# First transfers in another order, leftover taps as a whole-tile product, distances of two groups together

## The chip, the cores and the metric

The kernel runs on one core of a Trainium2 chip. The time is what the device takes for one execution, in microseconds (us); of several runs the median is given. The engines are named as in the profile: PE is the matrix engine (TensorE), PEld its weight loads, DVE the vector engine, ACT the scalar engine, POOL is GpSimd, and SP the engine that mostly issues transfers (DMAs).

## The reference, cut to what matters

Two graph layers work on 128 graphs of 128 nodes with 256 features, all in float32. Each is followed by a residual and a layer norm.

```python
# layer 0
norm  = (sum(adj, -1) + 1e-6) ** -0.5
f_hom = adj @ ((x @ theta) * norm) * norm
f_het = x @ W_h
gate  = sigmoid(x @ W_t + b_t)
x     = layernorm(x + elu(gate * f_hom + (1 - gate) * f_het))
# layer 1; xc = x transposed: channels, nodes
h      = relu(bn1(conv1d(xc, conv1_w)))             # one tap
x_conv = relu(bn2(conv1d(h, conv2_w, pad=8)) + xc)  # 17 taps over the nodes
s      = x @ w_se.T + b_se                          # three coordinates per node
dist   = sq[:, None] + sq[None, :] - 2 * s @ s.T    # sq: squared length of s
msg    = relu(x @ w_msg.T + b_msg)
x_nmp  = (exp(-dist) * adj) @ msg
x      = layernorm(x + gru([x_conv, x_nmp], x))     # gates r, z, n
```

The adjacency is dense in form: 128 matrices of 128x128.

## The kernel before

There are three stages.

**Stage A** (to about 720 us) goes over the 64 pairs of graphs in a loop over t, with each pair's work spread over several rounds: `l0_turn(t+1)` transposes the inputs (xT_ps) and sums degrees (deg), `l0_project(t)` makes f_ps and gate_ps, `l0_mix(t)` applies the adjacency (mix_ps), `l1_turn(t-2)` transposes the normed result (x1T_ps), `l1_front` is the one-tap convolution, and `l1_analyse` turns its result into coefficients over 136 frequencies (coef_ps). The 17-tap convolution is done as products per frequency. Therefore the weights conv2_w have to be turned into frequencies too, and stage A does this beside its other work. `w_load`, `w_unit` and `w_store` do 128 of the 136 rows, with four groups of 17 taps on four 32-row parts of PE (w_ps). `v_load`, `v_unit` and `v_store` do the leftover eight. There, seven input channels at a time (FS = 7, 7 x 17 = 119 rows) are multiplied with TL, a table with blocks for each channel (wl_ps, 56 rows out), in 19 units. TL is put together in `way_back` from table T by 14 small DMAs that POOL issues (L247). The layer norm's and the degree's power of -1/2 (`inv_sqrt`, L161 and L162) is also on POOL.

What sets the order: up to round 2 a scheduler decides, except on PE, where the order written in the code holds; from round 3 on the code's order holds for PE, SP, DVE and ACT. [...] Before the first round, SP gets `load(0)`, the gate weights, conv1's weights, `load(1)`, `w_load(0)` and `w_load(1)`. `load(p)` brings x and adjT of pair p.

**Stage B** (to about 912 us) multiplies by frequency (y_ps, z_ps).

**Stage C** (to the end) goes over 32 groups of four graphs, where PE's order is the code's and the rest is scheduled. For a group g, `l1_own` takes coordinates for the distances (every fourth group it transposes 16 graphs' worth, turn_ps, into `turned`, and each group scales them by a mask into `own`); `l1_kernel` multiplies `turned` and `own` on four 32-row parts of PE (dist_ps), takes exp(-dist) on ACT and multiplies with the adjacency on DVE (AT). `l1_project` makes the messages (msg_ps), `l1_gather` sums them by AT (nmp_ps), `l1_synth` goes back from frequencies to nodes for two groups (conv_ps), and `l1_gru` makes the gates for two graphs at a time (pr = 0, 1) in seven products (g_ps, three matmul kinds each) that go through four PSUM banks and are summed up by DVE and POOL. `l1_kernel(g + 1)` is put before the fifth product of `l1_gru(g, 1)`. Its PSUM tile takes four banks, which it shares in turn with `l1_synth`.

Of the kernel before, what the change touches and what calls it, by code (L numbers as in the profile page):

```python
# [9 lines left out]
F32 = mybir.dt.float32  # L10
I32 = mybir.dt.int32
AF = mybir.ActivationFunctionType
ALU = mybir.AluOpType

P = 128
D = 256
NC = D // P
J = 2
G = 4
TAPS = 17  # L20
# [7 lines left out]
ML = M - P  # L28
# [6 lines left out]
def gnn_layers_kernel(ctx: ExitStack, tc: tile.TileContext, a: dict, out: bass.AP):  # L35
# [10 lines left out]
    nc = tc.nc  # L46
    x, adjT = a["x"], a["adjT"]
# [35 lines left out]
    taps = actx.enter_context(tc.tile_pool(name="taps", bufs=1, side="right", reuse_waits="tile"))  # L83
# [4 lines left out]
    SL = const.tile([P, P], F32, tag="SL", name="SL")  # L88
    T = taps.tile([P, M], F32, tag="T", name="T")
    FS = P // TAPS  # L90
    TL = taps.tile([P, ML * FS], F32, tag="TL", name="TL")
    conv1_w = acon.tile([P, NC, D + CO], F32, tag="conv1_w", name="conv1_w")
    shift1 = acon.tile([P, D], F32, tag="shift1", name="shift1")
    NW = 3
    wt = [taps.tile([P, 2, D], F32, tag=f"wt{i}", name=f"wt{i}") for i in range(NW)]


# [15 lines left out]
    def load(p):  # L113
        s = st[p] = {}
        s["x"] = io.tile([P, J, D], F32, tag="x", name=f"x_{p}")
        nc.sync.dma_start(s["x"], x[p * J : (p + 1) * J].rearrange("b n d -> n b d"))
        s["adjT"] = io.tile([P, J, P], F32, tag="adjT", name=f"adjT_{p}")
        nc.sync.dma_start(s["adjT"], adjT[:, p * J : (p + 1) * J, :])
# [4 lines left out]
    def w_load(u):  # L123
        t = wt[u % NW]
        for r in range(4):
            f = r * QF + 2 * u
            nc.sync.dma_start(
                t[32 * r : 32 * r + TAPS], a["conv2_wT"][f : f + 2].rearrange("i t o -> t i o")
            )
# [16 lines left out]
    for i, q in enumerate("vmgb"):  # L146
        for k in range(2):
# [2 lines left out]
                vec[r : r + NC], a[f"L1_gnn_bn{k + 1}_{q}"].rearrange("(c p) -> c p", p=P)  # L150
            )

    nc.sync.dma_start(conv1_w[:, :, 0:D], a["conv1_wT"].rearrange("(c p) e -> p c e", p=P))
    nc.sync.dma_start(conv1_w[:, :, D:], a["w_seT"].rearrange("(c p) e -> p c e", p=P))
    load(1)
    w_load(0)
    w_load(1)

    def inv_sqrt(dst, src, eps, width):

# [74 lines left out]
    def way_back():  # L235

        AL = setup.tile([P, P // ML, ML], F32, tag="AL", name="AL")
        nc.vector.tensor_copy(AL, A[:, P:M].unsqueeze(1).to_broadcast([P, P // ML, ML]))
        nc.vector.memset(TL, 0.0)
        back = setup.tile([P, 1], F32, tag="back", name="back")  # L240
        nc.vector.memset(back, 2.0 / L)
        nc.vector.memset(back[0:2], 1.0 / L)

        cols = TL.rearrange("p (r i k) -> p r i k", r=2, i=FS)
        for i in range(FS):
            for r in range(2):
                nc.gpsimd.dma_start(  # L247
                    cols[i * TAPS : (i + 1) * TAPS, r, i, :], T[0:TAPS, P + r : M : 2]
                )
        tS = bank("S_ps")  # L250
        nc.tensor.transpose(tS[:, 0:P], A[:, 0:P], ident)
        nc.tensor.transpose(tS[:, P : 2 * P], AL.rearrange("p a b -> p (a b)"), ident)
        nc.vector.tensor_scalar(S, tS[:, 0:P], back, None, ALU.mult)
        nc.vector.tensor_scalar(SL, tS[:, P : 2 * P], 2.0 / L, None, ALU.mult)
# [185 lines left out]
    def v_sets(v):  # L440

        return [(f, min(FS, D - f)) for f in range(2 * FS * v, min(2 * FS * (v + 1), D), FS)]

    def v_load(v):
        t = taps.tile([P, 2, D], F32, tag="vt", bufs=2, name=f"v_t_{v}")
        for i, (f, n) in enumerate(v_sets(v)):
            nc.sync.dma_start(
                t[0 : n * TAPS, i, :], a["conv2_wT"][f : f + n].rearrange("i t o -> (i t) o")
            )
        s_v[v] = t  # L450

    def v_unit(v):
        n, sets = v_sets(v)[-1][1] * TAPS, len(v_sets(v))
        pl = bank(f"wl_ps_{v}")
        nc.tensor.matmul(  # L455
            pl[0 : ML * FS, 0 : sets * D], lhsT=TL[0:n],
            rhs=s_v[v][0:n, 0:sets].rearrange("p i o -> p (i o)"), start=True, stop=True,
        )
        ol = s_v[v] = taps.tile([ML * FS, 2, D], F32, tag="wl", name=f"wl_o_{v}")
        nc.vector.tensor_copy(  # L460
            ol[:, 0:sets].rearrange("p i o -> p (i o)"), pl[0 : ML * FS, 0 : sets * D]
        )
# [48 lines left out]
    for t in range(-1, NP):  # L511
        with tc.manual_schedule(engines={E.PE, E.SP, E.DVE, E.Activation} if t > 2 else {E.PE}):

            def on(q, work):
                if 0 <= q < NP:
                    work(q)

            def between():
                on(t - 1, l0_gate)
                on(t - 3, l1_analyse)  # L520

            def beside():
                on(t - 1, l0_elu)

            on(t - 2, l1_turn)
            l0_project(t, between, beside) if t >= 0 else between()
            on(t - 1, l0_norm)
            if t == 0:
                norms = batch_norms()
                next(norms)  # L530
                table(A, node, "A")
                table(T, lag, "T")

                cos, sin = T[:, 2:M:2], T[:, 3:M:2]
                both = setup.tile([P, M // 2 - 1], F32, tag="both", name="both")
                nc.vector.tensor_sub(both, sin, cos)
                nc.vector.scalar_tensor_tensor(sin, sin, -1.0, cos, ALU.mult, ALU.subtract)
                nc.vector.tensor_copy(cos, both)
            on(t - 2, l1_front)
            on(t - 2, l1_store)  # L540
            if t + 2 < NP:
                if 2 <= t + 2:
                    load(t + 2)
            else:
                m_load(t + 2 - NP)
            if t - 1 in units:
                w_store(units[t - 1])
            if t - 1 in units_v:
                v_store(units_v[t - 1])
            on(t + 1, l0_turn)  # L550
            if t == 2:
                v_load(0)
            if t == 3:
                nc.scalar.dma_start(w_msg, a["w_msgT"].rearrange("(c p) e -> p c e", p=P))
                nc.scalar.dma_start(b_msg, a["L1_gnn_b_msg"].partition_broadcast(P))
            if t == 1:
                next(norms, None)
                way_back()
                sctx.close()
                hpool = hstack.enter_context(tc.tile_pool(name="hpool", bufs=1))  # L560
                H = hpool.tile([P, NC, M, NB], F32, tag="H", name="H")
            on(t, l0_mix)
            if t in units_v:
                if units_v[t] + 1 < NV:
                    v_load(units_v[t] + 1)
                v_unit(units_v[t])
            if t in units:
                if units[t] + 2 < NU:
                    w_load(units[t] + 2)
                if t + 1 < NP:  # L570
                    w_unit(units[t])
# [299 lines left out]
        )  # L871
        st[g].update(turned=turned, own=own)

    def l1_kernel(g):
        s = st[g]
        turned, own = s["turned"], s["own"]
        pd = acc.tile([P, G, 512], F32, tag="acc", name=f"dist_ps_{g}")
        for q in range(G):
            k = slice(q * P // G, (q + 1) * P // G)
            nc.tensor.matmul(  # L880
                pd[:, q, 0:P], lhsT=turned[k, 0, :], rhs=own[k, :], start=True, stop=True
            )
        AT = ck.tile([P, G * P], F32, tag="AT", name=f"AT_{g}")
        nc.scalar.activation(
            AT.rearrange("p (q n) -> p q n", q=G), pd[:, :, 0:P], AF.Exp, scale=-1.0
        )
        nc.vector.tensor_mul(AT, AT, s["adjT"].rearrange("p q n -> p (q n)"))
        s["AT"] = AT


    def l1_gather(g):
# [115 lines left out]
    with tc.manual_schedule(engines={mybir.EngineType.PE}):  # L1007
        load_c(0)
        load_c(1)
        load_y(0)  # L1010
        for g in range(2):
            load_x1(g)
            l1_own(g)
        l1_project(0)
        l1_kernel(0)
        l1_project(1)
        l1_factors()
        l1_synth(0)
        for g in range(NG):
            d = g // 2  # L1020
            if g + 2 < NG:
                load_c(g + 2)
                if g % 2 == 0:
                    load_y(d + 1)
                load_x1(g + 2)
            l1_gather(g)
            if 2 <= g + 1 < NG:
                l1_own(g + 1)
                l1_project(g + 1)
            l1_gru(g, 0)  # L1030
            if g % 2 == 1 and d + 1 < ND:
                l1_synth(d + 1)
            if g + 1 < NG:
                l1_gru(g, 1, {4: lambda: l1_kernel(g + 1)})
    with tc.manual_schedule(engines={E.PE, E.DVE, E.Activation}):
        l1_gru(NG - 1, 1)
    cctx.close()
# [41 lines left out]
```

## Time and profile before

| | |
|---|---|
| median of three runs | 2053.21 us (2051.23 to 2053.49) |
| profiled execution | 2053.39 us |
| its span, first to last instruction | 2051.6 us |
| granted PE clock, mean | 0.995 |
| DMA rate over the span | 118 GB/s |
| PE in 0 to 50 us | 37.10 us busy, granted clock 0.86 |
| PE in 50 to 720 us (stage A) | 670.00 us busy |
| PE in 735 to 912 us (stage B) | 175.82 us busy |
| PE in 912 to 2051 us (stage C) | 1127.32 us busy |

The profile is of one execution. Busy time counts what an engine executes, not the waits; a float32 matmul of the code appears as two passes in the records. A form such as `32*128 32x128` gives the tile of the array that is used, and the streamed operand. In the view of waits, a row gives who waited for whom, the total in us, how often, and the longest.

### The profile page before, as it was taken

The page shows a single profiled execution, that of the slowest core. Times are in us where ns is not written, and L with a number is a line of the kernel's source. Part 1 is how long each engine was busy: PE and PEld are TensorE (multiplying, and loading weights), DVE is VectorE, ACT ScalarE, POOL GpSimd, SP SyncE. Part 2 cuts the span into 40 slices and gives each one's busy share as a digit, 9 for nine tenths or more (in the row PEclk, how much of TensorE's full clock was granted, in tenths as well). Part 3 has the DMA queues.
Part 4 walks back from the last instruction along what each step waited for, and adds up shares of the span by engine and source line. Part 5 has one row for each costly group of instructions (what it writes and reads, how often), then busy time and mean ns, then how long its engine had stood idle before and what let it go on. Part 6 is the DMA issues. An engine that isn't in the chain of part 4 may idle for free.

```text
span 2051.6 us, 27050 instructions
## 1 busy us (share of the span) xinstructions
PE 2023.9 (99%) x8807; PEld 1384.2 (67%) x8807; DVE 1432.1 (70%) x2882; ACT 746.4 (36%) x1488; POOL 652.0 (32%) x869
## 2 busy tenths in 40 slices
PE   7999999999999999999999999999999999999997
PEld 4666766766766788886666666666666666666664
DVE  5777777777777764456767677676667767776766
ACT  2555655655555621112222222222322222232222
POOL 4111111111111135553433334333424333342431
PEclk8999999999999999999999999999999999999999
DMA  4544444444444479994222122222212222121100
GB/s 96 170 153 149 142 154 150 141 156 152 141 153 146 133 269 359 313 306 147 72 74 79 52 66 81 63 66 64 79 61 70 73 67 63 58 79 52 42 26 21
DMA packets 198044, 243.04 MB, mean 118 GB/s; under 512 B 16768, under 2 KB 141456, under 8 KB 197904
## 3 DMA queue, kind: packets, MB, share of 16 engines
q1 hardware_dynamic: 190880, 235.47, 35.3%
q10 hardware_dynamic: 6352, 5.78, 0.9%
q0 software_dynamic: 672, 0.06, 0.4%
q8 instruction: 71, 1.16, 0.3%
q14 instruction: 69, 0.57, 0.1%
HBM read 136.33 MB, written 104.86 MB: 118 GB/s over the span
## 4 chain that ended last, share of the span: by engine, by line
PE 96%; DVE 2%; POOL 1%; DMA 1%; ACT 0%; issue 0%; POOLq 0%; DVEq 0%; ACTq 0%; SPq 0%
PE g_ps L964 42%; PE f_ps L317 11%; PE conv_ps L387 5%; PE gate_ps L322 5%; PE msg_ps L844 5%; PE y_ps L708 5%; PE mix_ps L343 3%; PE coef_ps L407 3%; PE nmp_ps L897 3%; PE conv_ps L808 3%; PE z_ps L721 3%; PE x1T_ps L284 2%; PE w_ps L423 2%; PE xT_ps L284 1%; PE deg L297 1%; PE wl_ps L455 1%
## 5 line engine op out<-in xcount | busy, mean ns | idle before, releaser
L317 PE MATMUL f_ps<-w,xT 128*128 128x512 f32 x512 | 244.4, 600 | 0.1
L923 ACT ACTIVATE o<-o 128x1024 f32<-128x1024 f32 (+1 forms) x65 | 67.8, 1044 | 326.8 <-DVE o L1000 269.7
L161 POOL TENSOR_SCALAR rstd_b<-mv_b 128x2 f32<-128x2 f32 (+1 forms) x65 | 18.2, 280 | 529.6 <-DVE mv_b L262 529.6
L964 PE MATMUL g_ps<-t_h,sh 128*128 128x384 f32 x384 | 158.4, 494 | 0.0
L964 PE MATMUL g_ps<-t_c,sc 128*128 128x384 f32 x384 | 155.2, 486 | 0.0
L964 PE MATMUL g_ps<-t_m,sm 128*128 128x384 f32 x384 | 155.2, 486 | 0.0
L161 POOL TENSOR_SCALAR rstd_a<-mv_a 128x2 f32<-128x2 f32 x64 | 12.3, 193 | 436.4 <-DVE mv_a L262 380.1
L322 PEld LDWEIGHTS gate_ps<-w,xT 128*128 128x128 f32 x512 | 98.3, 192 | 69.1 <-issue 61.8
L322 PE MATMUL gate_ps<-w,xT 128*128 128x256 f32 x512 | 132.6, 382 | 0.0
L997 POOL TENSOR_TENSOR u<-u,p 128x512 f32<-128x512 f32 x63 | 79.8, 1267 | 163.3 <-DVE p L981 163.3
L317 PEld LDWEIGHTS f_ps<-w,xT 128*128 128x128 f32 x512 | 89.0, 193 | 62.9 <-issue 62.3
L708 PE MATMUL y_ps<-wb,H 128*128 128x256 f32 x544 | 128.5, 379 | 0.9 <-ACT H L411 0.8
L326 ACT ACTIVATE hom<-f_ps,norm 128x256 f32<-128x256 f32 x128 | 60.7, 474 | 187.6 <-PE f_ps L317 182.3
L271 ACT ACTIVATE y<-y,nb_b,rstd_b 128x256 f32<-128x256 f32 x128 | 70.0, 593 | 157.8 <-DVE nb_b L269 157.8
L387 PE MATMUL conv_ps<-conv_w,x1T 128*128 128x259 f32 x512 | 122.5, 381 | 0.0
L716 POOL TENSOR_TENSOR ws<-wb 128x512 f32<-128x512 f32 x67 | 93.2, 1390 | 88.8 <-PE z_ps L721 53.5
L708 PEld LDWEIGHTS y_ps<-wb,H 128*128 128x128 f32 x544 | 103.2, 190 | 15.4 <-issue 1.4
L844 PE MATMUL msg_ps<-w_msg,cx1T 128*128 128x256 f32 x480 | 108.7, 379 | 0.0
L964 PEld LDWEIGHTS g_ps<-t_c,sc 128*128 128x128 f32 x384 | 73.0, 190 | 50.9
L964 PEld LDWEIGHTS g_ps<-t_m,sm 128*128 128x128 f32 x384 | 73.0, 190 | 50.9 <-DVE sm L912 0.2
L387 PEld LDWEIGHTS conv_ps<-conv_w,x1T 128*128 128x128 f32 x512 | 97.1, 190 | 14.7 <-ACT w_o L427 0.2
L964 PE MATMUL g_ps<-w_hhT_w,cx1T 128*128 128x384 f32 x256 | 105.0, 492 | 0.0
(228 smaller groups left out, 4524.8 us busy)
## 6 DMA issues: line engine op xcount, KB each, us to landing
wb<-w_d SPq DMA_DIRECT2D x68, 512.0 KB
w_d<-w_o SPq DMA_DIRECT2D x256, 128.0 KB
y_d<-yb SPq DMA_DIRECT2D x68, 256.0 KB
x<-in_x SPq DMA_DIRECT2D x64, 256.0 KB
cx1T<-x1T_d SPq DMA_DIRECT2D x64, 256.0 KB
yt<-y_d SPq DMA_DIRECT2D x32, 512.0 KB
cx<-x_d SPq DMA_DIRECT2D x32, 512.0 KB
x_d<-x SPq DMA_DIRECT2D x63, 256.0 KB
```

Of the source, the lines that this page charges most:

```text
L271: nc.scalar.activation(dst[:, q, :], src[:, q, :], AF.Identity, bias=nb[:, q : q + 1], scale=rstd[:, q : q + 1],)
L284: nc.tensor.transpose(t[:, (c * J + j) * P : (c * J + j + 1) * P], src[:, j, c * P : (c + 1) * P], ident,)
L317: nc.tensor.matmul(pf, lhsT=xT[:, c, nodes(j)], rhs=w0[:, c, 0 : 2 * D], start=(c == 0), stop=(c == NC - 1),)
L322: nc.tensor.matmul(pg[:, j * D : (j + 1) * D], lhsT=xT[:, c, nodes(j)], rhs=w0[:, c, 2 * D : 3 * D], start=(c == 0), stop=(c == NC - 1),)
L343: nc.tensor.matmul(pm[:, j * D : (j + 1) * D], lhsT=adjT_[:, j, :], rhs=hom[:, j, :], start=True, stop=True,)
L387: nc.tensor.matmul(ph[:, 0 : D + CO], lhsT=s["x1T"][:, c, nodes(j)], rhs=conv1_w[:, c, :], start=(c == 0), stop=(c == NC - 1),)
L708: nc.tensor.matmul(py[:, blk, :], lhsT=coefs(blk if k == 0 else 2 * k + 1 - blk, c), rhs=w[:, c, blk, :], start=(c == 0), stop=(c == NC - 1),)
L716: nc.gpsimd.tensor_tensor(ws, w[:, :, 0, :], w[:, :, 1, :], ALU.add)
L844: nc.tensor.matmul(pm[:, j * D : (j + 1) * D], lhsT=x1T[:, c, nodes(q)], rhs=w_msg[:, c, :], start=(c == 0), stop=(c == NC - 1),)
L923: nc.scalar.activation(rz, rz, AF.Tanh, scale=0.5)
L964: nc.tensor.matmul(pg[:, lo : lo + 3 * P], lhsT=s[f"f{kind}"][i][:, pr, :], rhs=factors[kind][i], start=(k == 0), stop=(k == 2), skip_grou ...
L997: nc.gpsimd.tensor_tensor(u4, u2, p5, add)
```

## The change

It has three parts.

First, `load(1)` comes before conv1's weights; `w_load(0)` and `w_load(1)` go into rounds 0 and 1, behind `load(2)` and `load(3)`; `v_load(0)` and `v_load(1)` go into rounds 2 and 3, and `v_load(v + 2)` comes after `v_unit(v)` instead of `v_load(v + 1)` before it. The `v_load` of unit v + 2 writes the buffer that unit v has just read.

Second, TL grows from 56 to 128 columns (zeros beyond the 56), the inputs get two fixed tiles `vt` whose last rows are set to zero once, and `v_unit` multiplies all 128 rows by all 128 columns; only the 56 rows of the result are read, as before.

Third, `l1_kernel` takes two groups. It puts the second group's distances in the columns beside the first's in the same four banks, and it is called for groups 0 and 1 at the start and then within `l1_gru(g, 1)` of odd g alone, for g + 1 and g + 2. `l1_own` is called one group earlier and before `l1_gather`, and AT has three buffers.

```diff
-    TL = taps.tile([P, ML * FS], F32, tag="TL", name="TL")
+    TL = taps.tile([P, P], F32, tag="TL", name="TL")
...
+    vt = [taps.tile([P, 2, D], F32, tag=f"vt{i}", name=f"vt{i}") for i in range(2)]
...
+    load(1)
     nc.sync.dma_start(conv1_w[:, :, 0:D], a["conv1_wT"].rearrange("(c p) e -> p c e", p=P))
     nc.sync.dma_start(conv1_w[:, :, D:], a["w_seT"].rearrange("(c p) e -> p c e", p=P))
-    load(1)
-    w_load(0)
-    w_load(1)
...
         nc.vector.memset(TL, 0.0)
+
+        for t in vt:
+            nc.vector.memset(t[96:], 0.0)
...
-        cols = TL.rearrange("p (r i k) -> p r i k", r=2, i=FS)
+        cols = TL[:, 0 : ML * FS].rearrange("p (r i k) -> p r i k", r=2, i=FS)
...
     def v_load(v):
-        t = taps.tile([P, 2, D], F32, tag="vt", bufs=2, name=f"v_t_{v}")
+        t = vt[v % 2]
...
     def v_unit(v):
-        n, sets = v_sets(v)[-1][1] * TAPS, len(v_sets(v))
+        sets = len(v_sets(v))
         pl = bank(f"wl_ps_{v}")
         nc.tensor.matmul(
-            pl[0 : ML * FS, 0 : sets * D], lhsT=TL[0:n],
-            rhs=s_v[v][0:n, 0:sets].rearrange("p i o -> p (i o)"), start=True, stop=True,
+            pl[:, 0 : sets * D], lhsT=TL, rhs=vt[v % 2][:, 0:sets].rearrange("p i o -> p (i o)"),
+            start=True, stop=True,
         )
...
                 if 2 <= t + 2:
                     load(t + 2)
+                if 0 <= t < 2:
+                    w_load(t)
+                if 2 <= t < 4:
+                    v_load(t - 2)
...
-            if t == 2:
-                v_load(0)
...
             if t in units_v:
-                if units_v[t] + 1 < NV:
-                    v_load(units_v[t] + 1)
                 v_unit(units_v[t])
+                if units_v[t] + 2 < NV:
+                    v_load(units_v[t] + 2)
...
-    def l1_kernel(g):
-        s = st[g]
-        turned, own = s["turned"], s["own"]
-        pd = acc.tile([P, G, 512], F32, tag="acc", name=f"dist_ps_{g}")
-        for q in range(G):
-            k = slice(q * P // G, (q + 1) * P // G)
-            nc.tensor.matmul(
-                pd[:, q, 0:P], lhsT=turned[k, 0, :], rhs=own[k, :], start=True, stop=True
+    def l1_kernel(*groups):
+
+        pd = acc.tile([P, G, 512], F32, tag="acc", name=f"dist_ps_{groups[0]}")
+        for i, g in enumerate(groups):
+            turned, own = st[g]["turned"], st[g]["own"]
+            for q in range(G):
+                k = slice(q * P // G, (q + 1) * P // G)
+                nc.tensor.matmul(
+                    pd[:, q, i * P : (i + 1) * P], lhsT=turned[k, 0, :], rhs=own[k, :],
+                    start=True, stop=True, skip_group_check=True,
+                )
+        for i, g in enumerate(groups):
+            AT = st[g]["AT"] = ck.tile([P, G * P], F32, tag="AT", bufs=3, name=f"AT_{g}")
+            nc.scalar.activation(
+                AT.rearrange("p (q n) -> p q n", q=G), pd[:, :, i * P : (i + 1) * P],
+                AF.Exp, scale=-1.0,
             )
-        AT = ck.tile([P, G * P], F32, tag="AT", name=f"AT_{g}")
-        nc.scalar.activation(
-            AT.rearrange("p (q n) -> p q n", q=G), pd[:, :, 0:P], AF.Exp, scale=-1.0
-        )
-        nc.vector.tensor_mul(AT, AT, s["adjT"].rearrange("p q n -> p (q n)"))
-        s["AT"] = AT
+            nc.vector.tensor_mul(AT, AT, st[g]["adjT"].rearrange("p q n -> p (q n)"))
...
         l1_project(0)
-        l1_kernel(0)
+        l1_kernel(0, 1)
         l1_project(1)
...
                 load_x1(g + 2)
+                l1_own(g + 2)
             l1_gather(g)
             if 2 <= g + 1 < NG:
-                l1_own(g + 1)
                 l1_project(g + 1)
...
             if g + 1 < NG:
-                l1_gru(g, 1, {4: lambda: l1_kernel(g + 1)})
+
+                l1_gru(g, 1, {4: lambda: l1_kernel(g + 1, g + 2)} if g % 2 == 1 else {})
```

More of the change, by code (lines that the diff above doesn't have):

```diff
@@ L449, in v_load @@
             )
-        s_v[v] = t
     def v_unit(v):
-        n, sets = v_sets(v)[-1][1] * TAPS, len(v_sets(v))
+        sets = len(v_sets(v))
         pl = bank(f"wl_ps_{v}")
         nc.tensor.matmul(
-            pl[0 : ML * FS, 0 : sets * D], lhsT=TL[0:n],
-            rhs=s_v[v][0:n, 0:sets].rearrange("p i o -> p (i o)"), start=True, stop=True,
+            pl[:, 0 : sets * D], lhsT=TL, rhs=vt[v % 2][:, 0:sets].rearrange("p i o -> p (i o)"),
+            start=True, stop=True,
         )
```

## The prediction

> **What bounds the kernel now.** I read the page first: the busy shares, then the chain that ended last.
>
> ```profile
> PE 2023.9 (99%) x8807; PEld 1384.2 (67%) x8807; DVE 1432.1 (70%) x2882; ACT 746.4 (36%) x1488; POOL 652.0 (32%) x869
> PE 96%; DVE 2%; POOL 1%; DMA 1%; ACT 0%; issue 0%; POOLq 0%; DVEq 0%; ACTq 0%; SPq 0%
> ```
>
> TensorE (PE) is busy for 2023.9 of 2051.6 us and makes 96% of the chain. A change can win in two ways only: it takes away PE's few waits, or it makes PE's own work shorter. So next the waits of PE, the two longest:
>
> ```profile
> PE xT_ps L284 <- DMA x<-in_x: 9.3, 2, 5.0
> PE x1T_ps L284 <- ACT x L271: 4.0, 3, 3.5
> ```
>
> Of the first row's 9.3 us, 4.3 are the start of the kernel, and 4.97 are a wait for the third pair of batches at 20.9 to 25.86 us. The 3.48 us of the second row end at 34.80. After 36 us PE hardly waits at all. To see what stands behind 34.80, the chain in order of time:
>
> ```profile
> 18.29 1.10 POOL TL L247
> 20.25 12.60 POOL TL L247 x12
> 32.93 0.20 POOL rstd_a L161
> 33.95 0.17 DVE nb_a L269
> 34.80 0.47 PE x1T_ps L284
> ```
>
> Fourteen small transfers into TL are issued by POOL, 1.06 us each, one right behind the other from 16.52 to 32.86 us, and the first layer norm's 1/sqrt on POOL is queued behind them. The third pair's late arrival is not in this chain.
>
> For PE's own work the timeline of PE. First a round with a product of leftover taps (wl_ps), then one without, where x1T follows mix at once. Columns: start, length, engine, line.
>
> ```profile
> 68.74 1.11 PE L343 MATMUL mix_ps<-hom,adjT 128*128 128x256 f32 x4
> 69.78 1.07 PE L455 MATMUL wl_ps<-v_t,TL 119*56 119x512 f32 x2
> 70.78 0.66 PE L284 MATMUL x1T_ps<-ident,x 128*128 128x128 f32 x4
> 71.27 1.88 PE L317 MATMUL f_ps<-w,xT 128*128 128x512 f32 x4
> ...
> 113.58 1.11 PE L343 MATMUL mix_ps<-hom,adjT 128*128 128x256 f32 x4
> 114.53 0.60 PE L284 MATMUL x1T_ps<-ident,x 128*128 128x128 f32 x4
> 114.96 1.88 PE L317 MATMUL f_ps<-w,xT 128*128 128x512 f32 x4
> ```
>
> From mix to f_ps it is 2.53 us with the product and 1.38 without: the product costs 1.15. Its two passes of 512 columns should cost 0.86 (f_ps, full tile: 71.27 to 72.99 for four, 0.43 each). So 0.29 us is lost at the edges where the tile goes from 128*128 to 119*56 and back. The same for the distances:
>
> ```profile
> 981.99 0.81 PE L964 MATMUL g_ps<-t_m,sm 128*128 128x384 f32 x2
> 982.73 0.50 PE L880 MATMUL dist_ps<-own,turned 32*128 32x128 f32 x8
> 983.16 0.91 PE L964 MATMUL g_ps<-t_h,sh 128*128 128x384 f32 x2
> 983.91 0.81 PE L964 MATMUL g_ps<-t_c,sc 128*128 128x384 f32 x2
> 984.55 0.81 PE L964 MATMUL g_ps<-t_m,sm 128*128 128x384 f32 x2
> ```
>
> Pairs of g_ps passes follow every 0.645 us, so 981.99 to 983.91 would take 1.29 without the distances; it takes 1.92. One group's distances cost 0.63: 0.10 on the way in, 0.43 themselves, 0.10 on the way out.
>
> **Part 1, order of the first transfers.** The second pair's x and adjacency go ahead of conv1's weights, and the first two w_loads (8 issues on SP, 7.08 us of its time from 8.59 on) go behind load(2) and load(3). SP then issues x of pair 2 near 8.6 instead of 15.72, so it is there long before PE asks at 20.73. The 4.97 us wait goes. What is late next: x1T of pair 0. PE's remaining work before it (transposes, degrees, row_ps, S_ps, mix) takes about 2.8 us, so it stands at x1T from about 23.5 us. POOL's order is unchanged; its first TL issue at 16.52 follows from the tables on DVE and from PE's vec_ps at 13.60, neither of which waits for a moved transfer. So x1T still starts at 34.80, and one wait of about 11 us stands where there were 4.97 and 3.48. Part 1 is worth 0.
>
> [...] The passes after the wait ran at half pace: xT_ps to mix_ps took 25.86 to 31.33, 5.5 us for 2.8 us of work. [...] The slow stretch after 34.80 (f_ps at 35.99 takes 3.62 for four, otherwise 1.88) stays, since PE has idled longer, not shorter. [...]
>
> What else moves: two memsets of 32x512 at the head of DVE; a DVE pass over 128x512 takes 0.69, so at most 1.4 us, against 0.89 idle there and 1.71 and 1.05 idle further on before the tables matter. The w_loads land by about 20 us and are used at 47.29 and 58.53. v_load(v+2) now waits on SP for the product v; behind it stands the store of x1T, which is copied after that product anyway. Cost 0; without the cover, a product would wait for some us once.
>
> **Part 2, whole tile for the leftover taps.** 19 products. The passes keep their 512 columns (256 in the last), so the 0.86 stays, and the 0.29 goes if a whole tile follows whole tiles as f_ps does after x1T. The longer weight load (190 ns against 128) lies under mix's pass of 216. 19 x 0.287 (the third digit from the starts of the single passes) = -5.45 us. Ends: 0 if the edges have another cause, -5.5.
>
> **Part 3, distances of two groups at once.** 16 pairs instead of 32 groups. A pair costs the edges once and four waves (of four 32-row tiles) instead of two. What is a further wave worth? The tile views of w_ps and dist_ps, the same 32-row form with 512 and 128 columns:
>
> ```profile
> L423 PE MATMUL w_ps<-wt,T x256: 587/640/692, 47.3 to 717.8; 17*128 17x512 f32 x128
> L880 PE MATMUL dist_ps<-own,turned x256: 270/321/372, 916.4 to 2004.6; 32*128 32x128 f32 x128
> ```
>
> Half the passes are longer by 105 and 102 ns: the first wave shows its weight load, the second doesn't. So a further wave costs its stream alone, 0.107 (w_ps: 0.427 for 512 columns). A pair then takes 0.10 + 0.43 + 2 x 0.107 + 0.10 = 0.846 against 2 x 0.632 = 1.265: 0.42 saved, times 16 = -6.7 us. [...]
>
> Off PE, at odd groups DVE now does two AT multiplies (0.68 each) and two own scalings (0.25 each) together before it sums product 4 (p<-g_ps, at 985.40 in the round shown). That sum ends near 987.3 instead of 986.1. PE next needs that bank for the second nmp_ps, at about 989.96: 2.7 us of cover. The two Exp on ACT take 0.60 each, and ACT idles 6.25 us after the first there. The adjacency of the second group is needed one group earlier; its load was issued at 985.29 for group 5, whose pair now comes at about 1050. The eight turn_ps pairs only move. Cost 0.
>
> **Sum.** 0 - 5.45 - 6.7 = -12.15 us. The profiled execution took 2053.39, 0.18 above the median of the runs. 2053.39 - 12.15 = 2041.2; against the median 2041.1.
>
> **Rivals.** (A) The forecast, 2041.1: 64%. (B) Loads of further waves are exposed as the rule says: 2053.2 - 5.45 - 3.3 = 2044.5: 14%. For it: the case with more than two waves in a row is not in the trace. (C) Part 1 pays, because the TL chain is not what it seems and x1T follows the third pair: up to 7.7 more, 2033.5, half of it 2037: 7%. Against it: POOL's 12.60 us without a gap. (D) The whole tile does not remove its edges, that is, the change does not do what it says: 2046.5: 6%. If the pairs fail as well, 2053: 3%. Against: mix to x1T at 113.58 shows no edge between whole tiles. (E) Slower: DVE becomes the bound in odd groups. If the two Exp come late behind an activation of 1.04 and a norm of 1.09 on ACT and the sum of product 4 is delayed by more than the 2.7 us of cover, PE waits for the bank in each of 15 pairs. It wins back all from 0.81 us of wait per pair (12.15 / 15), so from 3.5 us of lateness on; at 1.2 us it is 2053.2 - 12.15 + 18 = 2059: 6%. For it: DVE lags 5 us behind PE at 981.80, after the convolution's outputs.
>
> **Numbers.** 2041.1 is the case A. The range 2037.0 to 2046.5 holds A, B, the mild half of C and most of D. A change under 0.2% (4.1 us) can't be told from none by this measurement. Faster is A to D: 0.91; same, where both tile edits fail: 0.03; slower 0.06.
>
> **What would show it.** wl_ps should read 128*128, with x1T 0.86 us after it. dist_ps should come x16 in 16 places, 0.65 us to the next g_ps, with a third and a fourth wave as short as the second. PE's wait for x<-in_x should fall to about 4.3, that for ACT x rise to about 11, with x1T still at 34.8. It is wrong if x1T starts well before or after 34.8, if PE waits in the odd groups, or if a pair takes 0.86 or more.

## The result, and the profile after

The median went from 2052.56 us (four runs, 2051.23 to 2053.49) to 2041.52 us (four runs, 2040.12 to 2043.36). The ratio is 0.9947, with a 95% interval of 0.993 to 0.9964. The forecast was 2041.1, in a range of 2037.0 to 2046.5. The profiled execution took 2040.12 us, its span 2038.3 us, and the mean granted clock was 0.995 as before.

The page of the kernel after, its busy shares and the shares of the chain that ended last:

```profile
PE 2008.1 (99%) x8807; PEld 1387.0 (68%) x8807; DVE 1445.5 (71%) x2884; ACT 745.9 (37%) x1488; POOL 645.2 (32%) x869
...
PE 96%; DVE 2%; POOL 1%; ACT 0%; issue 0%; DMA 0%; POOLq 0%; DVEq 0%; ACTq 0%
```

PE runs the same 8807 passes in 15.8 us less of busy time (2023.9 before). It is still 96% of the chain: nothing else has become the bound. DVE has two instructions more, the two memsets.

The two longest waits of PE, of the kernel after (total, times, longest):

```profile
PE x1T_ps L286 <- ACT x L273: 11.6, 3, 11.1
PE xT_ps L286 <- DMA x<-in_x: 4.2, 1, 4.2
```

The wait for the third pair's x is gone (9.3 in two waits before, 4.2 in one after), and the wait for ACT's x has grown from a longest of 3.5 to 11.1. The chain in order of time shows where that wait ends and why:

```profile
19.73 12.58 POOL TL L249 x12
...
32.38 0.20 POOL rstd_a L160
...
32.66 0.73 POOL rstd_a L161
...
33.60 0.61 ACT x L273
...
34.25 0.47 PE x1T_ps L286
```

POOL still issues the TL transfers without a gap until 32.3 us. The first layer norm comes right behind, and x1T starts at 34.25 us, 0.55 earlier than before. The twelve issues themselves begin 0.52 earlier (19.73 here, 20.25 before).

The timeline of PE after, first a round with leftover taps, then a pair of groups' distances:

```profile
67.97 1.11 PE L345 MATMUL mix_ps<-hom,adjT 128*128 128x256 f32 x4
68.92 1.02 PE L456 MATMUL wl_ps<-vt,TL 128*128 128x512 f32 x2
69.78 0.60 PE L286 MATMUL x1T_ps<-ident,x 128*128 128x128 f32 x4
70.21 1.02 PE L319 MATMUL f_ps<-w,xT 128*128 128x512 f32 x2
```
```profile
974.83 0.81 PE L970 MATMUL g_ps<-t_m,sm 128*128 128x384 f32 x2
975.57 0.73 PE L884 MATMUL dist_ps<-own,turned 32*128 32x128 f32 x16
976.23 0.91 PE L970 MATMUL g_ps<-t_h,sh 128*128 128x384 f32 x2
976.97 0.81 PE L970 MATMUL g_ps<-t_c,sc 128*128 128x384 f32 x2
```

From mix to f_ps it is now 2.24 us (70.21 - 67.97), 2.53 before. From wl_ps to x1T it is 0.86, which is two passes of 512 columns at 0.43 each, the pace of f_ps. For the distances, 974.83 to 976.97 is 2.14 us and holds two pairs of g_ps passes (1.29), so 0.85 for two groups. Before it was 0.63 for one.

In summary, from the starts of instructions in the two traces (us):

| stretch of the profiled execution | before | after | difference |
|---|---|---|---|
| start to the first leftover product | 69.78 | 68.92 | -0.86 |
| first to last leftover product | 637.83 | 632.55 | -5.28 |
| from there to the first turn_ps of stage C | 204.95 | 204.34 | -0.61 |
| stage C, first turn_ps to last g_ps | 1126.75 | 1120.25 | -6.50 |

These add up to -13.25 of the 13.27 us between the two profiled executions; the medians are 11.04 apart. Single executions of one kernel differ by up to 6 us (2031.49 to 2037.36 in the four of the kernel after with its TL issues split), so the rows of the changed stages say more than the total. The first row is not the worth of part 1: the first leftover product starts at 68.79 us in the kernel with part 3 alone and at 69.69 in the one with part 2 alone, both with the old order of transfers.

### The profile page after: what moved, and what is told of

It is laid out like the page before. It is cut to its first block, busy times and chain, and to the rows that moved or that the text cites. A ratio compares the mean times of both kernels' runs of the same rounds, so it can differ in the third digit from the quotient of the medians.

```text
span 2038.3 us, 26961 instructions
## 1 busy us (share of the span) xinstructions
PE 2008.1 (99%) x8807; PEld 1387.0 (68%) x8807; DVE 1445.5 (71%) x2884; ACT 745.9 (37%) x1488; POOL 645.2 (32%) x869
## 4 chain that ended last, share of the span: by engine, by line
PE 96%; DVE 2%; POOL 1%; ACT 0%; issue 0%; DMA 0%; POOLq 0%; DVEq 0%; ACTq 0%
PE g_ps L970 42%; PE f_ps L319 11%; PE y_ps L711 6%; PE conv_ps L389 5%; PE gate_ps L324 5%; PE msg_ps L847 5%; PE mix_ps L345 3%; PE coef_ps L409 3%; PE nmp_ps L903 3%; PE conv_ps L811 3%; PE z_ps L724 3%; PE x1T_ps L286 2%; PE w_ps L425 2%; PE xT_ps L286 1%; PE deg L299 1%; PE conv_ps L818 1%
## 5 line engine op out<-in xcount | busy, mean ns | idle before, releaser
L160 POOL TENSOR_SCALAR rstd_b<-mv_b 128x2 f32<-128x2 f32 (+1 forms) x65 | 12.5, 192 | 529.9 <-DVE mv_b L264 529.9
```

## The experiments

The theory to test was that of the prediction. Parts 2 and 3 each pay by PE edges removed (an edge is what PE loses on its way between products of different tile form), and part 1 pays nothing, since TL's issues on POOL set the start of x1T. The rival was that part 1 pays and that the tile edits pay less. Where a median of before is given, it was measured on the same chip beside the kernel.

### One part at a time

**The first transfers alone**: the kernel before with part 1.

```diff
...
+    load(1)
     nc.sync.dma_start(conv1_w[:, :, 0:D], a["conv1_wT"].rearrange("(c p) e -> p c e", p=P))
     nc.sync.dma_start(conv1_w[:, :, D:], a["w_seT"].rearrange("(c p) e -> p c e", p=P))
-    load(1)
-    w_load(0)
-    w_load(1)
...
+                if 0 <= t < 2:
+                    w_load(t)
+                if 2 <= t < 4:
+                    v_load(t - 2)
...
-            if t == 2:
-                v_load(0)
...
-                if units_v[t] + 1 < NV:
-                    v_load(units_v[t] + 1)
                 v_unit(units_v[t])
+                if units_v[t] + 2 < NV:
+                    v_load(units_v[t] + 2)
```

> The kernel before with the first part alone, the order of the transfers. Theory (the start hangs on POOL's fourteen TL transfers): the wait for the third pair's x (4.97 us) goes, the wait at x1T grows to about 11 us, x1T of pair 0 still starts at 34.2 to 34.8 us, and the time is that of before within 0.7 us. Rival (the third pair's arrival costs 4.97 us and 2.7 us of slow clock): x1T starts near 27 to 30 us and the time falls by 5 to 7.7 us.

Measured: 2052.48 us against 2052.34 before; ratio 1.0001 [0.9993, 1.0009]. The waits of PE, and POOL's timeline:

```profile
PE x1T_ps L282 <- ACT x L269: 11.6, 3, 11.1
PE xT_ps L282 <- DMA x<-in_x: 4.3, 1, 4.3
```
```profile
20.62 12.61 POOL L245 DMA_DIRECT2D TL<-T  x12
33.30 0.19 POOL L159 TENSOR_SCALAR rstd_a<-mv_a 128x2 f32<-128x2 f32 x1
```

The 4.97 us wait is removed and comes back in front of x1T: two waits of 8.45 us together have become one of 11.05. The 2.6 us between them are the half pace of the passes from xT_ps to mix_ps (granted clock 0.50 from 24.05 to 30.87 us before), which has gone too and has been waited away as well. The twelve issues take the same 12.6 us, and the norm stands directly behind them. Part 1 alone is worth nothing, within 0.1% either way.

**The leftover taps alone**: the kernel before with part 2.

```diff
...
-            pl[0 : ML * FS, 0 : sets * D], lhsT=TL[0:n],
-            rhs=s_v[v][0:n, 0:sets].rearrange("p i o -> p (i o)"), start=True, stop=True,
+            pl[:, 0 : sets * D], lhsT=TL, rhs=vt[v % 2][:, 0:sets].rearrange("p i o -> p (i o)"),
+            start=True, stop=True,
...
```

> The kernel before with the second part alone, leftover taps by a whole tile. Theory (edges between tile shapes cost 0.287 us per product): wl_ps to x1T_ps 0.86 instead of 1.00 us, mix to wl_ps 0.216 instead of 0.309, in all 5.45 us less. Rival (the 11 us of the whole change come mostly from the pairs and the start): 0 to 2 us less.

Measured: 2047.31 us; ratio 0.9975 [0.9965, 0.9985], so about 5.1 us less. From the first to the last leftover product it is 632.55 us, to the hundredth as in the kernel with all three parts; stage C stays at 1126.75.

**The pairs alone**: the kernel before with part 3.

```diff
...
-        l1_kernel(0)
+        l1_kernel(0, 1)
...
-                l1_gru(g, 1, {4: lambda: l1_kernel(g + 1)})
+                l1_gru(g, 1, {4: lambda: l1_kernel(g + 1, g + 2)} if g % 2 == 1 else {})
```

> The kernel before with the third part alone, distances of two groups at once. Theory (a further wave of four row tiles costs its stream of 0.107 us, the edges are paid once): 0.41 us less for each of 16 pairs, 6.5 us in all. Rival (weight loads of further waves are exposed): 0.21 us per pair, 3.3 us in all. Rival (DVE in odd groups): no gain, PE waits in stage C.

Measured: 2045.92 us; ratio 0.9968 [0.9956, 0.998], so about 6.6 us less. Stage C is 1120.25 us long, the leftover products' stretch is as before. The tile view of the distances in this kernel (min/median/max of one pass, ns):

```profile
L881 PE MATMUL dist_ps<-own,turned x256: 270/270/373, 914.9 to 1964.3; 32*128 32x128 f32 x128
```

The median has gone from 321 to 270. Before, half of the passes were long (372 against 270), those of the first of two waves. Now only the first of four waves is long, and the median falls on the short ones. The records of the kernel after show the same and the weight loads with it: at 975.57 the first four loads (181 ns) start with their own passes, which take 372; the loads of the other three waves (184 to 187 ns) start while earlier passes run, and their passes take 270.

The three parts alone give about 0, -5.1 and -6.6 us, together -11.7; the whole change gave 0.53% [0.36, 0.7], or 10.9 us. They add, within what the interval allows (7 to 14 us).

### Which edge did the leftover product pay for?

Part 2 changes two sizes at once: the rows in use from 119 to 128, and the columns from 56 to 128. Each of two kernels keeps one of the old sizes.

119 rows with 128 columns, the rest as after:

```diff
-            pl[:, 0 : sets * D], lhsT=TL, rhs=vt[v % 2][:, 0:sets].rearrange("p i o -> p (i o)"),
+            pl[:, 0 : sets * D], lhsT=TL[0 : FS * TAPS], rhs=vt[v % 2][0 : FS * TAPS, 0:sets].rearrange("p i o -> p (i o)"),
```

> The changed kernel, with the leftover taps by 119 rows and all 128 columns. If the edges come from the number of columns in use (56), they stay away: mix to wl_ps 0.216 us, wl_ps to x1T_ps 0.86 us. If they come from the rows, they are back: 0.309 and about 1.00 us.

128 rows with 56 columns, the rest as after:

```diff
-            pl[:, 0 : sets * D], lhsT=TL, rhs=vt[v % 2][:, 0:sets].rearrange("p i o -> p (i o)"),
+            pl[0 : ML * FS, 0 : sets * D], lhsT=TL[:, 0 : ML * FS], rhs=vt[v % 2][:, 0:sets].rearrange("p i o -> p (i o)"),
```

> The changed kernel, with the leftover taps by all 128 rows and 56 columns. If the edges come from the columns, they are back: mix to wl_ps 0.309 us, wl_ps to x1T_ps about 1.00 us, 5.4 us in all. If from the rows, they stay away: 0.216 and 0.86 us.

Measured, one execution each: 2040.25 us for 119 x 128, 2045.74 us for 128 x 56. The timelines of PE, first of 119 x 128, then of 128 x 56:

```profile
67.66 1.11 PE L345 MATMUL mix_ps<-hom,adjT 128*128 128x256 f32 x4
68.60 1.02 PE L456 MATMUL wl_ps<-vt,TL 119*128 119x512 f32 x2
69.47 0.60 PE L286 MATMUL x1T_ps<-ident,x 128*128 128x128 f32 x4
```
```profile
68.15 1.11 PE L345 MATMUL mix_ps<-hom,adjT 128*128 128x256 f32 x4
69.19 1.07 PE L456 MATMUL wl_ps<-vt,TL 128*56 128x512 f32 x2
70.19 0.66 PE L286 MATMUL x1T_ps<-ident,x 128*128 128x128 f32 x4
```

From mix to x1T it is 1.81 us with 119 rows, the same as with the whole tile (67.97 to 69.78), and 2.04 with 56 columns, the same as before (68.74 to 70.78). With 56 columns wl_ps begins 0.10 us later after mix, x1T 0.14 later after wl_ps, and x1T itself takes 0.06 more (0.66 for 0.60). All nineteen products say the same: from the first to the last it is 632.62 us with 119 rows (632.55 with the whole tile) and 637.83 with 56 columns (637.83 before). The edge belongs to the number of columns in use. The step from 128 to 119 rows costs nothing, so the zero rows of `vt` and the two memsets could be left out. Fewer rows were not tried in this product; the distances with their 32-row tiles do have edges (0.10 us on each side in the round at 982.73 before).

### What POOL's fourteen issues cost

If TL's issues are what holds x1T back, moving them behind the norm should start x1T earlier, and more so when part 1 has brought the third pair in. Both kernels issue eight of TL's fourteen transfers in round 1 and six in round 2, with POOL's order in the first rounds as written.

```diff
+    def fill_left(lo, hi):
+        cols = TL[:, 0 : ML * FS].rearrange("p (r i k) -> p r i k", r=2, i=FS)
+        for i in range(lo, hi):
+            for r in range(2):
+                nc.gpsimd.dma_start(
+                    cols[i * TAPS : (i + 1) * TAPS, r, i, :], T[0:TAPS, P + r : M : 2]
+                )
...
-        for i in range(FS):
-            for r in range(2):
-                nc.gpsimd.dma_start(
-                    cols[i * TAPS : (i + 1) * TAPS, r, i, :], T[0:TAPS, P + r : M : 2]
-                )
+        fill_left(0, 4)
...
-        with tc.manual_schedule(engines={E.PE, E.SP, E.DVE, E.Activation} if t > 2 else {E.PE}):
+        with tc.manual_schedule(engines={E.PE, E.SP, E.DVE, E.Activation} if t > 2 else {E.PE, E.Pool}):
...
+            if t == 2:
+                fill_left(4, FS)
```

On the kernel after:

> The changed kernel, with POOL's order held to the code's in the first rounds and six of the fourteen TL transfers put into round 2, so that the first norm's 1/sqrt comes before all TL transfers. Theory (x1T waits for POOL's queue alone): x1T of pair 0 starts near 26.4 us instead of 34.25, 7.9 us less than the changed kernel, and up to 2.7 us more if PE's clock does not drop in the shorter wait; about 2033.5 us, at best 2031. Rival (something else holds x1T, or the TL transfers now hold the second norm for as long): 0 to 3 us less.

On the kernel before:

> The kernel before, its order of transfers kept, with the same new order of the TL transfers on POOL. Theory: now the third pair's x (wait to 25.86 us) is what the start hangs on, PE goes from there to x1T without a second wait, at about 31.3 us instead of 34.80, 3.5 us less than before, up to 6.2 us less if no second slow stretch follows. With the run of the changed kernel under the same order this tells what the first part is worth once POOL is out of the way: about 4.5 us. Rival (the order of transfers is worth nothing in any case): x1T starts as early as in the changed kernel with that order, near 26.4 us.

Measured: on the kernel after 2034.81 us, ratio to before 0.9912 [0.9899, 0.9926], about 6.7 us less than after; on the kernel before 2046.73 us against 2052.75, ratio 0.9971 [0.996, 0.9981], 6.0 us less. The timeline of PE in the kernel after with its TL issues split:

```profile
25.46 0.33 PE L289 MATMUL x1T_ps<-ident,x 128*128 128x128 f32 x1 [1.84 <-ACT x L276]
...
39.78 1.40 PE L289 MATMUL x1T_ps<-ident,x 128*128 128x128 f32 x4 [3.55 <-ACT x L276]
40.97 3.62 PE L322 MATMUL f_ps<-w,xT 128*128 128x512 f32 x4
```

The first x1T starts at 25.46, 8.8 us earlier than in the kernel after. So POOL was the reason for 34.25. But not all of it stays. The second x1T now waits 3.55 us, and the passes behind it run at half pace (granted clock 0.51 from 37.6 to 44.5 us): f_ps takes 3.62 for four, otherwise 1.88, and x1T 1.40 for 0.60. Wait and half pace are 3.55 + 1.74 + 0.80 = 6.1 us. The chain of waits of this kernel says what was late:

```profile
28.81 0.25 ACT het L332
29.06 9.98 DMA x_d<-x
...
39.12 1.09 ACT x L276 x2
```

The store of the first pair's result (x_d), issued at 29.06, landed only at 39.04. The next norm writes the same single buffer and had to wait for it. The kernel before with the same split has another course:

```profile
24.71 1.09 PE L287 MATMUL xT_ps<-ident,x 128*128 128x128 f32 x4 [3.79 <-DMA x<-in_x]
...
30.29 0.90 PE L287 MATMUL x1T_ps<-ident,x 128*128 128x128 f32 x4
31.02 1.88 PE L320 MATMUL f_ps<-w,xT 128*128 128x512 f32 x4
```

There the third pair's x is waited for (3.79 us), and after that x1T comes without a wait at 30.29. Its one stretch at half pace lies ahead of that (x1T's 0.90 is the end of it). It is later than 25.46, yet the second wait of 3.55 us and the half pace behind it don't occur. So the two kernels gain nearly the same from the split. Between them lie about 12 us, and parts 2 and 3 alone gave 11.7: part 1, expected to be worth about 4.5 us here, is again worth nothing that shows.

### The store that was late next

The first pair's x_d store is put on ACT's queue, on top of the kernel after with the split; and the same again without part 1.

```diff
-        queue.dma_start(x1_d[p], s["x1"].rearrange("p j e -> p (j e)"))
+        (nc.scalar if p == 0 else queue).dma_start(x1_d[p], s["x1"].rearrange("p j e -> p (j e)"))
```

> The changed kernel with the new order of the TL transfers on POOL (as in the run before), and the store of the first pair's normed result sent from ACT's queue instead of SP's. In the run before, the second pair's norm waited until 39.08 us for that store, which SP had issued at 29.06 behind the w_loads and which took 10 us to land; the norm overwrites the buffer that it reads. Theory: on a queue of its own the store lands in about 3 us, x1T of pair 1 starts near 36.5 us instead of 39.78 and at full clock, 3.5 to 6 us less than the run before, about 2029 to 2031 us. [...]

> The same kernel with the first part undone: the order of transfers of the kernel before. Theory: with POOL and the store out of the way the third pair's x is what the start hangs on (wait to about 24.7 us, 3.8 us and 2.7 us of slow clock), x1T of pair 0 near 30.3 us as in the run of the kernel before with POOL's new order, and about 2035.3 us (2046.73 less 11.4 for the other two parts), 4 to 6 us more than the kernel beside it: that is then the worth of the first part. Rival (the first part is worth nothing even then): within 1 us of the kernel beside it.

Measured: with part 1 2034.38 us, ratio 0.991 [0.9896, 0.9925]; without it 2032.69 us, ratio 0.9902 [0.9885, 0.9918], both against 2052.37. The timeline of PE with the store moved, with part 1:

```profile
25.47 0.33 PE L289 MATMUL x1T_ps<-ident,x 128*128 128x128 f32 x1 [1.86 <-ACT x L276]
...
26.34 3.01 PE L322 MATMUL f_ps<-w,xT 128*128 128x512 f32 x4
29.15 1.64 PE L327 MATMUL gate_ps<-w,xT 128*128 128x256 f32 x4
...
37.86 0.66 PE L289 MATMUL x1T_ps<-ident,x 128*128 128x128 f32 x4
```

The second x1T no longer waits, and the first leftover product starts at 59.19 instead of 63.54. The median, though, is only 0.4 us below that of the split alone. The profiled execution gave 4 us back in stage B, which took 181.99 us instead of 178.16 (first y_ps to first turn_ps), and it was the longest of its four runs. Its trace shows where, first on DVE, then on PE:

```profile
847.98 1.48 DVE L697 TENSOR_TENSOR bias<-bias,bias_h 128x512 f32<-128x512 f32 x1 [4.62 <-DMA bias_h<-in_L_gnn_b_hh]
```
```profile
852.05 1.14 PE L729 MATMUL z_ps<-ws,hs 128*128 128x256 f32 x4 [2.25 <-DVE hs L726]
852.99 3.58 PE L716 MATMUL y_ps<-wb,H 128*128 128x256 f32 x8
```

DVE waited 4.62 us for the transfer of a bias (2.3 to 2.9 in every other trace), PE then 2.25 us for DVE, and the eight y_ps passes behind it ran at half pace (3.58 us for 1.89, granted clock 0.50 from 853.0 to 856.4). The transfer was issued at 840.34, more than 800 us after the moved store, and nothing of the edit reaches there. Why it landed late in this execution is open. The two medians don't tell the kernels apart.

Without part 1:

```profile
23.84 0.63 PE L291 MATMUL xT_ps<-ident,x 128*128 128x128 f32 x4 [2.50 <-DMA x<-in_x]
...
24.68 2.04 PE L231 MATMUL row_ps<-diag,ones 128*128 128x512 f32 x2
...
26.94 1.61 PE L350 MATMUL mix_ps<-hom,adjT 128*128 128x256 f32 x4
28.39 0.60 PE L291 MATMUL x1T_ps<-ident,x 128*128 128x128 f32 x4
```

PE waits 2.50 us for the third pair, has a short stretch at half pace, and goes from there to x1T without a wait: its first leftover product starts at 59.98, 0.8 us after the kernel with part 1. The median is 1.7 us lower, and the intervals overlap. Thus the theory that part 1 would pay 4 to 6 us once POOL is out of the way fell: no gain is shown. In the traces the wait that part 1 removes is partly replaced by the 1.86 us for ACT's x, and each kernel has one stretch at half pace at its start in either case.

This last kernel has the lowest median of all, below both kernels of the case: about 19.7 us under before. It can't be told apart from the two others with the split.

## Why the prediction was right, point by point

**What bounds the kernel.** PE's own work and a few waits at the start: confirmed. PE's share of the chain is unchanged, and after 60 us no wait of PE is longer than 1.3 us, in either kernel.

**Part 1, worth 0.** Right, and by the mechanism named. x1T stood at 34.80 before. It started at 35.18 in the kernel with part 1 alone and at 34.25 with all parts, after one wait of 11.05 us. The kernels without part 1 (taps alone, pairs alone) have 34.76 and 35.17, so this scatter is not part 1's. What x1T follows is POOL: it starts 14.52 to 14.56 us after the first of the twelve TL issues in all seven kernels that leave these on POOL in one run, with part 1 and without it. (The fourteen issues of before are not all one right behind the other: two steps of a norm, at 17.88 and 19.41 us, stand behind the first and the second. Only the last twelve run without a gap.) The 7.7 us of rival C (the wait of 4.97 and the 2.7 of half pace behind it) no run shows as a gain: with part 1 alone that wait and that half pace were both gone, and the median was 2052.48 us against 2052.34, since their time was waited away in front of x1T. What the prediction didn't see is what the POOL row itself was worth: 6.0 us in the kernel before, 6.7 in the kernel after.

**Part 2, -5.45.** Measured 5.28 us over the 18 intervals from first to last product, 0.293 each against 0.287; and 5.1 by the medians of part 2 alone. The cause was told too widely: "the tile goes from 128*128 to 119*56" names rows and columns, and only the columns pay.

**Part 3, -6.7.** Stage C became 6.5 us shorter, 0.41 a pair against 0.42. A pair takes 0.855 us, where 0.846 was worked out. The eight additional passes cost 0.657 - 0.433 = 0.224 us (dist_ps to the next g_ps, after and before), so 0.11 a wave; the bare stream was put at 0.107. No run shows the 3.3 us that rival B takes for the pairs: it is an estimate in which each further wave pays 0.107 for its load beside 0.107 for its stream, 0.43 us for the two. In this form, with four 32-row tiles in turn, the loads of the further waves lie under running passes (184 to 187 ns each, the passes 270 as in the second wave of before), the stage became 6.5 us shorter, and rival B is out.

**DVE as cover in odd groups (rival E).** The timeline of DVE, first of the kernel before behind the distances at 982.73, then of the kernel after behind the pairs at 975.57 and at 1042.69:

```profile
985.40 0.69 DVE L981 TENSOR_TENSOR p<-g_ps,bias 128x512 f32<-128x512 f32 x1
```
```profile
977.43 1.28 DVE L894 TENSOR_TENSOR AT<-AT,cadjT 128x512 f32<-128x512 f32 x2
978.63 0.69 DVE L987 TENSOR_TENSOR p<-g_ps,bias 128x512 f32<-128x512 f32 x1
...
983.01 1.01 DVE L872 TENSOR_SCALAR own<-turned,mask 128x128 f32<-128x128 f32 x2
...
1044.56 0.47 DVE L872 TENSOR_SCALAR own<-turned,mask 128x128 f32<-128x128 f32 x2
1044.94 1.29 DVE L894 TENSOR_TENSOR AT<-AT,cadjT 128x512 f32<-128x512 f32 x2
1046.15 0.68 DVE L987 TENSOR_TENSOR p<-g_ps,bias 128x512 f32<-128x512 f32 x1
```

Both AT multiplies stand before the sum of product 4 in every pair, as predicted. The two scalings into own stand there in every other pair only. Where turn_ps has to run first, they come behind the sum: the sum then ends 3.75 us after the first dist_ps pass, instead of 3.36 before. Without turn_ps they come ahead of it, as predicted, and it ends after 4.14. So it is 0.4 or 0.8 us later, not 1.2, and well within the cover of 2.7 us: after the first turn_ps PE shows no wait in stage C.

**The sum.** -12.15 was forecast. By stretches it is 11.8 us for parts 2 and 3 in the profiled execution, and 1.5 more in rows that no part claims; by the medians it is 11.04. So the change was 1.1 us smaller than forecast, below what the runs can tell (the interval goes from 7 to 14 us). That the median lies only 0.4 us from 2041.1 is luck in part: before's median fell by 0.65 us with a fourth run.

## What to carry to other kernels

Before a wait is credited to an edit, look for the next thing that the same engine waits for, on every queue. Here one 5 us wait stood in front of another one that ended at the same time regardless, and the row that mattered was a compute engine issuing small transfers ahead of a norm. For a product of odd shape, ask which of its sizes leaves the whole-array form: here a padding of the columns from 56 to 128 bought all of the 5.3 us, and that of the rows from 119 to 128 nothing that shows (632.55 us for 632.62). For narrow products, try them side by side: two groups' distances took 0.855 us together and 1.265 apart, since the edges were paid once.

## What the runs showed of the hardware

The number of columns alone made the edge: 56 columns cost 0.29 us per product between whole tiles, with 119 or with 128 rows (637.83 us from the first to the last product in both), and 119 rows with 128 columns cost nothing that shows (632.62, and 632.55 with the whole tile).

After a short wait PE ran at half pace in some runs and not in others. The first x1T waited 1.84 us in the kernel after with the split and 1.86 in the one with the store moved, at the same place (about 23.6 to 25.5 us). In the first the granted clock stayed at 1.00 (24.0 to 30.8 us), and f_ps followed at 1.88 us for four. In the second it was 0.50 from 27.0 to 30.4 us, f_ps took 3.01, and gate_ps 1.64 for 1.03. Behind the wait of 2.25 us (stage B, above) y_ps took 3.58 for 1.89, and behind that of 2.50 us (without part 1) row_ps took 2.04 for 1.10. The stretches at half clock near the start differed in length, too: 6.82 us twice in the kernel before (24.05 to 30.87 and 34.29 to 41.11), 13.65 in the kernel after (26.46 to 40.11), which begins within the wait of 11.1 us. So the length of a wait alone doesn't tell whether half pace follows; what does, these runs don't settle.

Small transfers took much of the DMA engines' time here. From 20 to 45 us in the kernel after with the split, by queue (packets, MB, share of 16 engines):

```profile
q0 software_dynamic: 574, 0.05, 30.3%
q1 hardware_dynamic: 1486, 1.91, 25.8%
```

POOL's queue, with TL, moved 0.05 MB and took 30.3% of the engines' time; SP's moved 1.91 MB in 25.8%. The x_d store took its 9.98 us within that stretch. Whether TL's packets or the transfers ahead of it in its own queue delayed it was not tried apart. In the kernel with the store moved, eight TL issues run beside the store just the same, and its last packet on ACT's queue ends at 32.50 us, 5.7 us after its issue. That speaks for SP's queue as a part of the 9.98 us, but the store went out 2.3 us earlier there.
